# A graph network on one Trainium2 core: VectorE's sums moved ahead of the reads of PSUM

## The chip, the cores and the metric

The kernel runs on one core of a Trainium2 chip. The metric is the device time of a whole execution in microseconds (us), as a median of several runs. A profile is one execution taken by the hardware profiler; its times are counted from the first instruction, and its span (631.9 us) is a little shorter than the execution's time (633.71 us), which also covers what lies around the instructions.

The engines are named as in the profile: PE is TensorE (matmul; PEld is its weight load), DVE is VectorE, ACT is ScalarE, POOL is GpSimd, SP issues the transfers.

## The reference, cut to what matters

`x` has 16 batches of 1024 nodes with 64 features, `adj` is 1024 x 1024, all float32. Layer 0 is an attention whose softmax runs over the queries and whose scores are multiplied by `adj`; layer 1 adds up five terms with `adj` and its square.

```python
# layer 0
Q, K, V = x @ Wq.T + bq, x @ Wk.T + bk, x @ Wv.T
score = softmax(einsum('bnc,bmc->bnm', Q, K), axis=1)
x = layernorm(x + einsum('bnm,bmc->bnc', einsum('bnm,mc->bnc', score, adj), V))
# layer 1, with both supports equal to adj
x_stack = [x]
for support in (adj, adj):
    x1 = einsum('ij,bjk->bik', support, x)
    x2 = 2.0 * einsum('ij,bjk->bik', support, x1) - x
    x_stack += [x1, x2]
x = layernorm(x + einsum('bnf,fo->bno', concatenate(x_stack), weight) + bias)
```

The kernel folds the weights of layer 1 first, so that layer 1 is two products with `adj`, called hop 1 and hop 2 here. `Y` is multiplied by `adj` and added to `U` (hop 1); the sum is multiplied by `adj` again and added to a third term (hop 2); a layer norm and the output follow. One more such product, ahead of the attention, is not touched.

## The kernel before: the parts that matter

Each hop is a product of a 1024 x 1024 matrix (left, `adj`) and a 1024 x 1024 matrix (right, nodes by batches and features). It is done with seven products of quarters in place of eight (Strassen's scheme in Winograd's form): sums of quarters of the left matrix (`S`) and of the right one (`T`) are made by VectorE, the seven products by TensorE, and each product is added to one or two quarters of the result. Products 2, 3 and 4 are split once more in the same way, into seven *parts* each; VectorE makes their eight inner sums (`halves`). Products 1, 5, 6 and 7 are done in two *groups* (`g` = 0 and 1) of eight matmuls.

The sums wait in one list. `later` puts them there, `fill(n)` takes out the first n and issues them on VectorE, `need` issues until those named are out.

```python
    line = []
    def later(name, pieces):
        line.extend((name, piece) for piece in pieces)
    def fill(n):
        for _ in range(min(n, len(line))):
            line.pop(0)[1]()
    def need(*names):
        while any(name in names for name, _ in line):
            fill(1)
```

A group is multiplied into a PSUM tile of two banks; then VectorE reads the tile, adding it to the result (`take`). A part goes into one bank of two tiles (`two_tiles`). Parts 1, 6, 7 and 4 use the same bank and parts 6, 7 and 4 add to what is in it, so part 6 has to wait until part 1 has been read, and so on; part 2 uses the other tile's first bank, parts 5 and 3 its second.

```python
        def take(self, pt, block, n, pair, m):
            # ... cut: cells and views ...
            if cells <= self.seen:
                nc.vector.tensor_add(at(self.res), got, at(self.res))
            elif self.plus is None:
                nc.scalar.activation(at(self.res), got, AF.Copy)
            else:
                nc.vector.tensor_add(at(self.res), got, at(self.plus))
            self.seen |= cells

        def targets(self, name):              # which quarters of the result
            return {
                1: [(0, 0)], 2: [(0, 0)], 3: [(0, 1)], 4: [(1, 0)], 6: [(0, 1)],
                5: [(1, 1)] + [(0, 1)] * (3 in self.twice),
                7: [(1, 1)] + [(1, 0)] * (4 in self.twice),
            }[name]

        def step(self, name, g, fills=0, rows=(0, 1)):
            self.matmuls(name, g, rows)       # tiles[g] for 1, 6, 7, 4; tiles[2 + g] for 2, 3, 5
            self.read(name, g, rows)
            fill(fills)

        def part(self, name, q, two_tiles):
            a, b = self.sub[q]
            tile_, bank = {1: (0, 0), 6: (0, 0), 7: (0, 0), 4: (0, 0), 2: (1, 0)}.get(q, (1, 1))
            pt = two_tiles[tile_][:, ts(bank, H)]
            # ... cut: four matmuls of 128 x 256 into pt ...
            self.take(pt, i * HB + 2 * di, 2, c * NP // 2 + 2 * dc, 2)

    PARTS = (1, 2, 6, 5, 7, 3, 4)
```

Hop 1 begins while the attention's last normalisation and weights are done (`weigh`, `transposed`), with products 1 and 2; products 5, 3, 6 and 7 are in `turns`, which both hops use; product 4 comes last.

```python
    hop_1.read(1, 0)
    two = (h[2], h[3])
    hop_1.part(2, 1, two)
    fill(1)
    hop_1.part(2, 2, two)
    fill(1)
    transposed(p, h[1])
    # ... cut: parts 6 and 5 with fill(1), parts 7, 3, 4 without, and weigh between them ...
    need("S1")
    line[:0] = [("T1", f) for f in hop_1.right_sum(1)]
    hop_1.step(1, 1, 7)
    two = (h[1], h[3])
    SUB_DONE = {2: (0, 0), 7: (1, 1), 3: (0, 1), 4: (1, 0)}

    def turns(product, room, after_5, after_6):
        S = product.S
        need("S1", "T1")
        lefts, rights = product.halves(3, room[0])
        later("half", [f for both in zip(lefts, rights) for f in both])
        for g in range(2):
            product.step(5, g, 6)
        need("half")
        later("T2", product.right_sum(2))
        later("T3", product.right_sum(3))
        for q in PARTS:
            product.part(3, q, two)
            fill(1)
        need("S2", "T2")
        if after_5:
            later("S3", left_sum(S, 3))
        lefts, rights = product.halves(4, room[1])
        later("half", lefts)
        for g in range(2):
            product.step(6, g, 5)
            after_6(g)
        need("S3", "T3")
        later("T4", product.right_sum(4))
        later("half", rights)
        for g in range(2):
            product.step(7, g, 4 if after_5 else 5)
            if not after_5:
                leave(1, 1, g)
        need("half")
```

A *leave* is the end of the layer norm for rows and columns of the result that are complete: ScalarE squares them, VectorE reduces the squares, the inverse root is made by GpSimd (`inverse_root`) or by ScalarE and VectorE (`inverse_root_2`), GpSimd (the last one: VectorE) multiplies, SP sends. All behind the square is put at the front of the list of sums.

```python
    def leave(i, c, g, half=None):
        # ... cut: r, the rows ...
        nc.scalar.activation(sq, r, AF.Square)
        def rest():
            engine = nc.gpsimd
            if half is not None and i:
                rstd = inverse_root_2(rows, 2 * nb)
                if (g, half) == (1, 0):
                    engine = nc.vector
            else:
                rstd = inverse_root(row_sums(rows, 2 * nb), 2 * nb)
            # ... cut: the product with rstd on engine, and two transfers out ...
        line.insert(0, ("leave", rest))

    # hop 2
    for g in range(2):
        hop_2.step(1, g, 6)
    need("half")
    for q in PARTS:
        hop_2.part(2, q, two)
        fill(1)
        if q in SUB_DONE:
            leave(0, 0, *SUB_DONE[q])
    turns(hop_2, room[::-1], False, lambda g: leave(0, 1, g))
    for q in PARTS:
        hop_2.part(4, q, two)
        fill(1)
        if q in SUB_DONE:
            leave(1, 0, *SUB_DONE[q])
    need("leave")
```

Of the kernel before, what the change touches and what calls it, by code (L numbers as in the profile page):

```python
# [18 lines left out]
def gnn_kernel(  # L19
# [31 lines left out]
    def ps_tile(name):  # L51
        return ps.tile([P, 2 * H], FP, tag="ps", name=name)
# [182 lines left out]
# [11 lines that stand above are left out]
    class Product:  # L246
# [87 lines left out]

        def step(self, name, g, fills=0, rows=(0, 1)):
            self.matmuls(name, g, rows)
            self.read(name, g, rows)
            fill(fills)

        def halves(self, name, room):  # L340

# [20 lines left out]
            ]  # L362
            return lefts, rights

        def part(self, name, q, two_tiles):


            a, b = self.sub[q]
            tile_, bank = {1: (0, 0), 6: (0, 0), 7: (0, 0), 4: (0, 0), 2: (1, 0)}.get(q, (1, 1))
            pt = two_tiles[tile_][:, ts(bank, H)]  # L370
            start = q in (1, 2, 5)
            W = H // 2
            for i in range(2):
                for k in range(2):
                    nc.tensor.matmul(  # L375
                        pt[:, ts(i, W)], a[:, k, ts(i, P)], b[:, :, k],
                        start=(start and i == k == 0), stop=(k == 1), skip_group_check=True,
                    )
            (i, c), = self.targets(name)
            di, dc = {1: (0, 0), 2: (0, 0), 6: (0, 1), 3: (0, 1), 7: (1, 1), 5: (1, 1), 4: (1, 0)}[q]  # L380
            self.take(pt, i * HB + 2 * di, 2, c * NP // 2 + 2 * dc, 2)

    PARTS = (1, 2, 6, 5, 7, 3, 4)
# [9 lines left out]
    def scores(n):  # L393

        p, m = steps[n]
        sc = [ps_tile(f"sc{j}") for j in range(2)]
        for h in range(2):
            for j in range(2):
                s = slice(j * C, (j + 1) * C)
                nc.tensor.matmul(  # L400
                    sc[j][:, ts(h, H)], GY[s, p, ts(m, P)], xT[s, p, ts(h, H)],
                    start=True, stop=True,
                )
        NM[n] = small.tile([P, 2], FP, tag="nm", name="nm")
        E[n] = att.tile([P, 2, N], FP, tag="e", name="e", bufs=3)
        for j in range(2):
            nc.vector.tensor_scalar(  # L407
                E[n][:, j], sc[j], -1.0, None, op0=ALU.mult, op1=ALU.min,
                accum_out=NM[n][:, j : j + 1],
            )  # L410
        SM[n] = small.tile([P, 2], FP, tag="es", name="es")

    def exponentials(n, j):
        nc.scalar.activation(  # L414
            E[n][:, j], E[n][:, j], AF.Exp, bias=NM[n][:, j : j + 1], scale=-1.0,
            accum_out=SM[n][:, j : j + 1],
        )

    def scaled(n):

        p, m = steps[n]
        ri = small.tile([P, 2], FP, tag="ri", name="ri")
        nc.vector.reciprocal(ri, SM.pop(n))
        US[n] = small.tile([P, 2, C], FP, tag="us", name="us")
        nc.vector.tensor_tensor(  # L425
            US[n], U[:, m, ts(p, P)].rearrange("p (b c) -> p b c", b=2),
            ri[:, :, None].to_broadcast([P, 2, C]), ALU.mult,
        )

    def weighted(n):  # L430
        p, m = steps[n]
        if m == 0:
            ACC[p] = pacc.tile([P, N], FP, tag="acc", name="acc")
        es, us = E.pop(n), US.pop(n)
        for h in range(2):
            for j in range(2):
                nc.tensor.matmul(  # L437
                    ACC[p][j * C : (j + 1) * C, ts(h, H)], us[:, j], es[:, j, ts(h, H)],
                    start=(m == 0), stop=(m == K8 - 1),
                )  # L440
# [96 lines left out]
    for n, (p, m) in enumerate(steps):  # L537
        if p == NP - 1:
            if m == 0:
                later("half", [f for both in zip(*hop_1.halves(2, room[0])) for f in both])  # L540
            fill(1)
        if n + 2 <= last:
            scores(n + 2)
            exponentials(n + 2, 0)
        if p and m > 4:
            weigh(p - 1, m - 5)
        elif p > 1 and m == 0:
            weigh(p - 2, 3)
        if n + 1 <= last:
            scaled(n + 1)  # L550
        weighted(n)
        if m == K8 - 1:
            take(p)
        if n + 2 <= last:
            exponentials(n + 2, 1)
        if p:
            if m == 0:
                norm_1(p - 1)
            elif m == 1:
                norm_2(p - 1)  # L560
            elif m == 4:
                transposed(p - 1)
# [7 lines left out]
    h = [pacc.tile([P, N], FP, tag="acc", name="h0")] + [ps_tile(f"h{n}") for n in (1, 2, 3)]  # L570
# [7 lines left out]
    hop_1.read(1, 0)  # L578
    two = (h[2], h[3])
    hop_1.part(2, 1, two)  # L580
    fill(1)
    hop_1.part(2, 2, two)
    fill(1)
    transposed(p, h[1])
    hop_1.part(2, 6, two)
    fill(1)
    hop_1.part(2, 5, two)
    fill(1)
    weigh(p, 0, h[1])
    hop_1.part(2, 7, two)  # L590
    hop_1.part(2, 3, two)
# [7 lines left out]
# [11 lines that stand above are left out]
        for g in range(2):  # L610
            product.step(5, g, 6)
        need("half")
        later("T2", product.right_sum(2))
        later("T3", product.right_sum(3))
        for q in PARTS:
            product.part(3, q, two)
            fill(1)
        need("S2", "T2")
        if after_5:
            later("S3", left_sum(S, 3))  # L620
# [13 lines that stand above are left out]
# [5 lines left out]
    ])  # L639
    for q in PARTS:  # L640
        hop_1.part(4, q, two)
        fill(1)
    need("S1")

    def leave(i, c, g, half=None):

        first_block = i * HB + 2 * g
        nb, b0 = (B // 2, c * B // 2) if half is None else (B // 4, c * B // 2 + half * B // 4)
        r = R[:, first_block : first_block + 2, b0 * C : (b0 + nb) * C].rearrange(
            "p i (b c) -> p i b c", c=C  # L650
        )
        sq = att.tile([P, 2, nb, C], FP, tag="rT", name="sq2")
        nc.scalar.activation(sq, r, AF.Square)  # L653
        rows = sq.rearrange("p i b c -> p (i b) c")

        def rest():
            engine = nc.gpsimd
            if half is not None and i:
                rstd = inverse_root_2(rows, 2 * nb)
                if (g, half) == (1, 0):  # L660
                    engine = nc.vector
            else:
                rstd = inverse_root(row_sums(rows, 2 * nb), 2 * nb)
            engine.tensor_tensor(
                r, r, rstd.rearrange("p (i b) c -> p i b c", i=2), ALU.mult
            )
            for n in range(2):
                nc.sync.dma_start(out[ts(first_block + n, P), b0 : b0 + nb], r[:, n])

        line.insert(0, ("leave", rest))  # L670

    hop_2 = Product(S, by_pair(U), by_pair(R), hop_1.tiles, xT.rearrange("p q (k f) -> p q k f", k=K8), (2, 3, 4))
    later("T1", hop_2.right_sum(1))
    lefts, rights = hop_2.halves(2, room[0])
    later("half", [f for both in zip(lefts, rights) for f in both])
    for g in range(2):
        hop_2.step(1, g, 6)
    need("half")
    for q in PARTS:
        hop_2.part(2, q, two)  # L680
        fill(1)
        if q in SUB_DONE:
            leave(0, 0, *SUB_DONE[q])
    turns(hop_2, room[::-1], False, lambda g: leave(0, 1, g))
    for q in PARTS:
        hop_2.part(4, q, two)
        fill(1)
        if q in SUB_DONE:
            leave(1, 0, *SUB_DONE[q])
    need("leave")  # L690
# [40 lines left out]
```

## Time and profile before

| what | us |
|---|---|
| time, median of three runs | 633.69 (632.64 to 634.97) |
| span of the profiled execution | 631.9 |
| TensorE busy | 606.1 |
| VectorE busy | 391.5 |
| ScalarE busy | 226.2 |
| GpSimd busy | 84.2 |

A row of the profile has a line of the kernel, the engine, the operation, what it writes and reads, and the busy time; a bracket or a last column says how long the engine was idle just before and what ended that. In the rows that matter here, L322 is a matmul of a group, L375 of a part, L309 and L313 are reads of a product by VectorE, L276 sums of the right matrix, L224 of the left one, L356 to L361 the inner sums of a product that is split again. `h` is a PSUM tile of the products, `U`, `GY` are results, `S`, `T` and `xs` hold sums. A float32 matmul has two records in the trace, so the four matmuls of a part count as x8 and the eight of a group as x16. The clock row gives the clock that TensorE was granted, in tenths of full speed. Ends of matmuls are modelled by the profiler.

### The profile page before, as it was taken

The page shows a single profiled execution, that of the slowest core. Times are in us where ns is not written, and L with a number is a line of the kernel's source. Part 1 is how long each engine was busy: PE and PEld are TensorE (multiplying, and loading weights), DVE is VectorE, ACT ScalarE, POOL GpSimd, SP SyncE. Part 2 cuts the span into 40 slices and gives each one's busy share as a digit, 9 for nine tenths or more (in the row PEclk, how much of TensorE's full clock was granted, in tenths as well). Part 3 has the DMA queues.
Part 4 walks back from the last instruction along what each step waited for, and adds up shares of the span by engine and source line. Part 5 has one row for each costly group of instructions (what it writes and reads, how often), then busy time and mean ns, then how long its engine had stood idle before and what let it go on. Part 6 is the DMA issues. An engine that isn't in the chain of part 4 may idle for free.

```text
span 631.9 us, 6267 instructions
## 1 busy us (share of the span) xinstructions
PE 606.1 (96%) x2414; PEld 297.0 (47%) x2414; DVE 391.5 (62%) x706; ACT 226.2 (36%) x381; POOL 84.2 (13%) x47
## 2 busy tenths in 40 slices
PE   9999999999999999999999999999879989899974
PEld 7544444433344343443434344476355464646453
DVE  1695321267767777676776869653675575475584
ACT  4110100256666676676767666621000000100111
POOL 0000022400020303020030303000000000420373
PEclk9999999999999999999999999999989999899988
DMA  8600001000000000000000000000000000010023
GB/s 306 245 1 1 0 0 66 1 0 2 0 2 1 0 1 1 2 1 0 1 1 1 2 1 0 1 0 2 0 1 0 0 1 0 25 43 1 13 81 106
DMA packets 7917, 14.32 MB, mean 23 GB/s; under 512 B 2128, under 2 KB 4176, under 8 KB 7888
## 3 DMA queue, kind: packets, MB, share of 16 engines
q1 hardware_dynamic: 7568, 13.90, 6.1%
q8 instruction: 19, 0.31, 0.2%
q14 instruction: 10, 0.08, 0.0%
q10 hardware_dynamic: 320, 0.03, 0.0%
HBM read 9.73 MB, written 4.19 MB: 22 GB/s over the span
## 4 chain that ended last, share of the span: by engine, by line
PE 90%; DVE 7%; DMA 1%; issue 1%; ACT 1%; POOLq 0%; POOL 0%; ACTq 0%
PE h L322 32%; PE sc L400 20%; PE acc L437 19%; PE h L375 10%; PE pw L473 3%; PE po L452 2%; PE pt L109 2%; PE pg L131 2%; DVE U L309 1%; DVE GY L313 1%; DMA xs<-in_x_dram 1%; DVE xs L360 1%; DVE xs L361 1%; DVE xs L357 1%; PE h L473 1%
## 5 line engine op out<-in xcount | busy, mean ns | idle before, releaser
L407 DVE TENSOR_SCALAR_CACHE_REDUCE e<-sc 128x1024 f32<-128x1024 f32 x128 | 151.6, 1221 | 64.9 <-PE sc L400 64.9
L414 ACT ACTIVATE e<-e,nm 128x1024 f32<-128x1024 f32 x128 | 146.2, 1142 | 75.4 <-DVE e L407 75.2
L400 PE MATMUL sc<-xT,GY 64*128 64x512 f32 x512 | 128.5, 615 | 0.5 <-DVE e L407 0.5
L437 PE MATMUL acc<-e,us 128*64 128x512 f32 x512 | 124.0, 605 | 0.3 <-DVE us L425 0.3
L185 POOL TENSOR_TENSOR rstd<-var,expo 128x16 f32<-128x16 f32 (+1 forms) x15 | 40.0, 2664 | 433.6 <-DVE var L180 433.5
L322 PE MATMUL h<-T,S 128*128 128x512 f32 x192 | 83.6, 593 | 2.8 <-DVE T L276 2.0
L400 PEld LDWEIGHTS sc<-xT,GY 64*128 64x128 f32 x512 | 45.1, 186 | 73.3 <-issue 49.7
L309 DVE TENSOR_TENSOR U<-h,U 128x512 f32<-128x512 f32 (+1 forms) x39 | 36.1, 935 | 63.6 <-PE h L322 52.6
L653 ACT ACTIVATE sq<-GY 128x512 f32<-128x512 f32 (+1 forms) x12 | 9.2, 770 | 173.8 <-DVE GY L309 151.5
L437 PEld LDWEIGHTS acc<-e,us 128*64 128x64 f32 x512 | 31.1, 136 | 71.0 <-issue 61.3
L322 PEld LDWEIGHTS h<-T,S 128*128 128x128 f32 x192 | 36.4, 190 | 48.0 <-issue 46.3
L375 PE MATMUL h<-xs 128*128 128x256 f32 x144 | 39.1, 436 | 10.9 <-DVE GY L309 5.9
L322 PE MATMUL h<-S,aT 128*128 128x512 f32 x96 | 41.7, 593 | 0.0
L311 ACT ACTIVATE U<-h 128x1024 f32<-128x1024 f32 (+1 forms) x9 | 8.4, 928 | 91.4 <-PE h L322 91.4
L375 PEld LDWEIGHTS h<-xs 128*128 128x128 f32 x144 | 31.1, 220 | 18.4 <-DVE GY L309 7.1
L309 DVE TENSOR_TENSOR GY<-h,GY 128x512 f32<-128x512 f32 (+1 forms) x25 | 19.3, 772 | 24.8 <-PE h L322 13.1
L322 PEld LDWEIGHTS h<-S,aT 128*128 128x128 f32 x96 | 18.3, 190 | 22.9 <-issue 22.7
L526 POOL TENSOR_TENSOR xs<-xs,mu 128x1024 f32<-128x1024 f32 x8 | 15.0, 1903 | 102.6 <-DVE T L276 90.2
L322 PE MATMUL h<-xs,aT 128*128 128x512 f32 x64 | 27.6, 592 | 0.0
L473 PEld LDWEIGHTS pw<-raw,xT 64*128 64x128 f32 x224 | 19.2, 187 | 15.8 <-issue 5.8
L414 ACT ACTIVATION_READ_ACCUMULATOR e<-e,nm 128x1 f32 x128 | 24.0, 188 | 0.0
L473 PE MATMUL pw<-raw,xT 64*128 64x192 f32 x224 | 24.0, 332 | 0.0
(142 smaller groups left out, 578.0 us busy)
## 6 DMA issues: line engine op xcount, KB each, us to landing
aT<-in_adjT_dram SPq DMA_DIRECT2D x8, 512.0 KB, 11.2
xs<-in_x_dram SPq DMA_DIRECT2D x7, 512.0 KB, 6.6
out_dram<-GY SPq DMA_DIRECT2D x16, 128.0 KB, 2.0
out_dram<-GY SPq DMA_DIRECT2D x8, 256.0 KB, 2.2
aT<-in_adjT_dram SPq DMA_DIRECT2D x1, 1024.0 KB, 5.0
xs<-in_x_dram SPq DMA_DIRECT2D x2, 256.0 KB, 2.8
w1s<-in_w_dram SPq DMA_DIRECT2D x2, 80.0 KB, 9.9
wq<-in_wqT_dram ACTq DMA_DIRECT2D x2, 16.0 KB, 3.1
```

Source lines behind the costliest of these rows:

```text
L109: nc.tensor.transpose(pt[:, ts(k, P)], xs[:, p, k, :], ident)
L131: nc.tensor.matmul(pg[:, ts(h, H)], m_w, xT[:, p, ts(h, H)], start=True, stop=True)
L185: nc.gpsimd.tensor_tensor(rstd, var, expo[:, 0:g], ALU.pow)
L309: nc.vector.tensor_add(at(self.res), got, at(self.res))
L322: nc.tensor.matmul(pt[:, ts(i, H)], a[:, k, ts(2 * g + i, P)], b[:, :, k], start=(start and k == 0), stop=(k == HB - 1), skip_group_check= ...
L375: nc.tensor.matmul(pt[:, ts(i, W)], a[:, k, ts(i, P)], b[:, :, k], start=(start and i == k == 0), stop=(k == 1), skip_group_check=True,)
L400: nc.tensor.matmul(sc[j][:, ts(h, H)], GY[s, p, ts(m, P)], xT[s, p, ts(h, H)], start=True, stop=True,)
L407: nc.vector.tensor_scalar(E[n][:, j], sc[j], -1.0, None, op0=ALU.mult, op1=ALU.min, accum_out=NM[n][:, j : j + 1],)
L414: nc.scalar.activation(E[n][:, j], E[n][:, j], AF.Exp, bias=NM[n][:, j : j + 1], scale=-1.0, accum_out=SM[n][:, j : j + 1],)
L437: nc.tensor.matmul(ACC[p][j * C : (j + 1) * C, ts(h, H)], us[:, j], es[:, j, ts(h, H)], start=(m == 0), stop=(m == K8 - 1),)
L473: nc.tensor.matmul(pw[:, j, ts(k, 3 * C)], xT[s, p, ts(2 * c + k, P)], raw[s, 0:3].rearrange("p w c -> p (w c)"), start=True, stop=True,)
L526: nc.gpsimd.tensor_tensor(rows_of(p), rows_of(p), mu[:, p, :, None].to_broadcast([P, G, C]), ALU.subtract)
```

## The change

VectorE's queue is in the order of the program. Before, a sum was put into it behind the read of a group or part, so that it ran only after the matmuls of that group had ended, though VectorE had been idle during them. The change puts the sums ahead of the read, so that they run beside the matmuls. For hop 1's product 2 this gives each of the seven parts a sum, where four had one. In hop 2, product 1's second group goes between products 5 and 3, product 2's second and later parts get no single sums, and the first quarter's leaves are two of a whole group in place of four; two of the last four leaves take GpSimd's power in place of ScalarE's square root.

```diff
         def step(self, name, g, fills=0, rows=(0, 1)):
             self.matmuls(name, g, rows)
+            fill(fills)
             self.read(name, g, rows)
-            fill(fills)

-        def part(self, name, q, two_tiles):
+        def part(self, name, q, two_tiles, fills=1):
 ...
+            fill(fills)
             (i, c), = self.targets(name)
 ... the fill(1) behind every part is dropped; in the attention's last pair
 ... fill(1) moves from the head of a turn to just before weighted(n)

     def turns(product, room, after_5, after_6):
         for g in range(2):
             product.step(5, g, 6)
         need("half")
+        if not after_5:
+            product.step(1, 1, 1)
+            leave(0, 0, 1)
         later("T2", product.right_sum(2))

     def leave(i, c, g, half=None):
-            if half is not None and i:
+            if half is not None and i and g != half:
                 rstd = inverse_root_2(rows, 2 * nb)
-                if (g, half) == (1, 0):
+                if g:
                     engine = nc.vector

-    for g in range(2):
-        hop_2.step(1, g, 6)
+    hop_2.tiles = [h[0], h[2], h[3], h[1]]
+    hop_2.step(1, 0, 9)
+    hop_2.part(2, 1, two)
+    hop_2.part(2, 2, two)
     need("half")
-    for q in PARTS:
+    for q in PARTS[2:]:
         hop_2.part(2, q, two)
-        fill(1)
-        if q in SUB_DONE:
-            leave(0, 0, *SUB_DONE[q])
+    leave(0, 0, 0)
```

More of the change, by code (lines that the diff above doesn't have):

```diff
@@ L550, in gnn_kernel @@
             scaled(n + 1)
+        fill(1)
         weighted(n)
@@ L580, in gnn_kernel @@
     hop_1.part(2, 1, two)
-    fill(1)
     hop_1.part(2, 2, two)
-    fill(1)
     transposed(p, h[1])
     hop_1.part(2, 6, two)
-    fill(1)
     hop_1.part(2, 5, two)
-    fill(1)
     weigh(p, 0, h[1])
@@ L616, in turns @@
             product.part(3, q, two)
-            fill(1)
         need("S2", "T2")
@@ L641, in gnn_kernel @@
         hop_1.part(4, q, two)
-        fill(1)
     need("S1")
@@ L675, in gnn_kernel @@
     later("half", [f for both in zip(lefts, rights) for f in both])
-    for g in range(2):
-        hop_2.step(1, g, 6)
+    hop_2.tiles = [h[0], h[2], h[3], h[1]]
+    hop_2.step(1, 0, 9)
+    hop_2.part(2, 1, two)
+    hop_2.part(2, 2, two)
     need("half")
-    for q in PARTS:
+    for q in PARTS[2:]:
         hop_2.part(2, q, two)
-        fill(1)
-        if q in SUB_DONE:
-            leave(0, 0, *SUB_DONE[q])
+    leave(0, 0, 0)
     turns(hop_2, room[::-1], False, lambda g: leave(0, 1, g))
@@ L686, in gnn_kernel @@
         hop_2.part(4, q, two)
-        fill(1)
         if q in SUB_DONE:
```

## The prediction

> **What bounds the kernel now.** I read the page first: how busy each engine is, and where in the span TensorE (PE) is not.
>
> ```profile
> PE 606.1 (96%) x2414; PEld 297.0 (47%) x2414; DVE 391.5 (62%) x706; ACT 226.2 (36%) x381; POOL 84.2 (13%) x47
> ...
> PE   9999999999999999999999999999879989899974
> ...
> PEclk9999999999999999999999999999989999899988
> ```
>
> TensorE is busy 96% of the span, so nothing can be won but its gaps. They all lie in the last 190 us (slices 29 to 40), which are the two hops, and in three places the clock row dips too. The change touches just this stretch. Next, the waits of TensorE alone from 430 us to the end:
>
> ```profile
> PE h L375 <- DVE GY L309: 5.9, 3, 3.5
> PE h L375 <- DVE U L309: 5.7, 3, 2.8
> PE h L322 <- DVE T L276: 2.0, 1, 2.0
> PE h L322 <- DVE GY L309: 0.8, 1, 0.8
> PE h L375 <- DVE GY L313: 0.8, 1, 0.8
> ```
>
> Columns: total, times, longest. All nine waits, 15.1 us, are for VectorE: mostly for a read of a PSUM tile (L309, L313), once for a sum (L276). The timeline of TensorE says when; the bracket is the idle time ahead of the row:
>
> ```profile
> 445.40 13.97 PE L322 MATMUL h<-T,S 128*128 128x512 f32 x32 [2.01 <-DVE T L276]
> ...
> 461.82 2.00 PE L375 MATMUL h<-GY,S 128*128 128x256 f32 x8 [0.72 <-DVE U L309]
> 466.63 7.13 PE L375 MATMUL h<-xs 128*128 128x256 f32 x24 [2.81 <-DVE U L309]
> ...
> 510.26 5.45 PE L375 MATMUL h<-xs 128*128 128x256 f32 x24 [2.12 <-DVE U L309]
> ...
> 538.42 7.13 PE L375 MATMUL h<-xs 128*128 128x256 f32 x24 [2.07 <-DVE GY L309]
> ...
> 549.79 14.00 PE L322 MATMUL h<-T,S 128*128 128x512 f32 x32 [0.78 <-DVE GY L309]
> ...
> 566.29 2.00 PE L375 MATMUL h<-U,S 128*128 128x256 f32 x8 [0.77 <-DVE GY L313]
> 568.69 5.45 PE L375 MATMUL h<-xs 128*128 128x256 f32 x24 [0.41 <-DVE GY L309]
> ...
> 611.97 8.27 PE L375 MATMUL h<-xs 128*128 128x256 f32 x24 [3.45 <-DVE GY L309]
> ```
>
> A part shows as x8 and a group as x16. Three parts (x24) take 5.45 us behind the wait at 510.26, but 7.13 and 8.27 us behind three others. There the clock was at half:
>
> ```profile
> 466.00:467.00 1.00, 0.37 (x2) 1.00 0.00 0
> ...
> 468.00:469.00 1.00, 1.00 (x4) 0.50 0.00 0
> ```
>
> (The column before the last two is the granted clock.) What VectorE did ahead of 466.63, from its timeline:
>
> ```profile
> 459.41 2.35 DVE L309 TENSOR_TENSOR U<-h,U 128x1024 f32<-128x1024 f32 x2 [0.71 <-PE h L322]
> 461.68 0.68 DVE L360 TENSOR_TENSOR xs<-GY 128x512 f32<-128x512 f32 x1
> ...
> 465.89 0.68 DVE L309 TENSOR_TENSOR U<-h,U 128x512 f32<-128x512 f32 x1
> ```
>
> Seven sums, 461.68 to 465.89, stand between the read of product 5's second group and the read of part 1, and part 6 adds into part 1's bank, so it waits. It was idle 0.71 us just before, while TensorE ran: the sums are not too many, they are late.
>
> [...] The trace agrees on the half (0.50) and on its length (467.2 to 471.0, 539.4 to 542.7), but idle times of 2.07 and 2.81 us brought it, while 2.01 and 2.12 us did not[...]. [...] the trace has a sum (L357) of 1.53 us in place of 0.68 at 562.44, beside GpSimd's product of 562.28.
>
> **The units.** From consecutive starts in the timelines: a part 1.73 us (473.60, 475.32, 477.05), a group of eight matmuls 6.87 (477.05 to 490.78 for two); a VectorE sum or half-width read 0.60, a full read 1.14. A read starts 1.93 us after its part's start and 7.15 after its group's. A wait also costs some 0.16 us of drain (two parts at 504.52 show 3.62 against 3.46). So before, the nine waits cost 15.1 + 1.5 = 16.6 us, and the slow clock (6.97 - 5.19) twice, and 8.10 - 5.19: 6.5 us. In all TensorE loses 23.1 us there.
>
> **The change, part by part.** No matmul, read or sum is added or removed; only VectorE's order changes (one sum per read, ahead of it, a group's sums ahead of its read), product 1's second group moves, and the square roots and leaves of hop 2 are regrouped. I laid VectorE's new order against TensorE's with these units.
>
> Product 2, hop 1: the first S1 sum comes ahead of part 1's read, which ends at 424.18 and not 423.77; part 6 starts near 424.24, not 423.88. Loss 0.36. The parts now take three S2 sums as well.
>
> Product 5, hop 1: T1's four sums run from about 438 us, while product 1's second group is multiplied, and not after its read at 443.43. The 2.01 us wait goes; product 5 starts at 443.5.
>
> Product 3, hop 1: all eight sums are made before the last read of product 5. That read, two of 1.14 us, still holds part 2 back (it uses the same tile): the wait of 0.72 stays, 0.97 with drain. Part 1's read, one sum behind it, ends 0.5 us before part 6 can start. The wait of 2.81 and its slow window go.
>
> Product 4, hop 1: the four right sums come before product 7's second read. Behind it VectorE has 2.28 us of read, one sum (0.60) and part 1's read (0.68), against 3.46 us of parts 1 and 2: loss 0.46 in place of 2.12.
>
> Hop 2, products 1 and 2: nine pieces fit under the first group (from 513 or so, the read of product 4's last part, to 517.5: T1 2.4, five sums 3.0). Behind the read (1.14) come one sum and part 1's read: 2.4 us, under 3.46. The 2.07 wait and its slow window go.
>
> Product 1's second group now runs between products 5 and 3: 6.87 us in which product 5's second read (2.28) is done, so the 0.77 and 0.41 waits go, and the leaves that stood before product 5 (0.78) too. But its own read (1.23) is followed by a new thing: ScalarE's square (1.06), the reduction of it on VectorE (1.24 with the small scale) and only then part 1's read (0.68), as VectorE's queue is in order. 7.15 + 1.23 + 1.06 + 1.24 + 0.2 + 0.75 = 11.6 us from the group's start, against 6.87 + 3.46 = 10.3: new loss 1.2.
>
> Product 4, hop 2: before, two reads (2.27), a reduction, four sums and part 1's read gave the wait of 3.45. Now the sums come before the reads, but the square of the last leave (1.06) is waited for, with its reduction (1.3); the first reads begin 0.4 us late behind the sums. Loss 2.8 with drain, in place of 3.6.
>
> The end: the last part's read waits for a reduction, square root and reciprocal of the leave before it, some 1.2 us behind its matmuls; then 3.4 us of square, reduction, root and product, against 4.28 before (623.83 to 628.11), and the same 3.8 us to the end. From the last matmul that is 0.2 us longer.
>
> Losses after: 0.36 + 0.97 + 0.46 + 1.2 + 2.8 = 5.8. To this I add 0.5[...] and 1.4 for the clock at 2.8 us of idle[...]. With 0.2 for the end: 7.9 in place of 23.1, so 15.2; walking the starts forward instead gave 15.8. I take 15.5: 633.7 - 15.5 = 618.2 us.
>
> **Rivals.** First: the waits only move. A sum ahead of a read delays that read, and TensorE waits for reads; with every read so delayed 0.6 us, some 30 parts would cost 18 us and the kernel would be near 634. Against it: a part gives VectorE 1.73 us and it needs 1.2, and its timeline shows idle times of 0.44 ahead of the reads even now. Second: the leaves become the bound. A square and reduction between two reads costs 2.4 us at each of three places; the gain would shrink to 10 or so, 624 us. For it: GpSimd takes 3 us a power, and it and ScalarE sit inside the chain; against: only two places have a read behind them at once. Third: the slow clock stays at random places; two more slow windows make 621.7. Fourth: every wait including the last goes, with no slow window: 614.
>
> **Range and chances.** The first five places follow from order alone, and I trust them to 1 us together; the end is worth 2 us either way, a window 1.8. Eight times in ten between 615.4 and 622.0. Faster by over 2% means below 621.0; 2.8 us of error in one direction is needed to miss it: 0.84. Within 2%: 0.15. Slower: 0.01, as no added work is on the path.
>
> **What would show it.** In the changed trace TensorE's waits should be four or five, 5 to 6 us together, none over 1.5 before 590 us; no wait for T; product 5 of hop 1 at 443.5; the clock at half once at most, near 597 us; VectorE's sums of a group ended before its read. I am wrong if parts 6 or 2 wait at other places than those named, if the square of a leave holds VectorE over 1.5 us, or if the clock is at half twice.

## The result, and the profile after

The changed kernel takes 617.91 us (median of four, 616.33 to 619.28) against 634.33; the ratio is 0.973 (0.967 to 0.979). Run again beside the experiments it took 615.71 against 633.41, 0.972 (0.969 to 0.975). The span of its first profile is 617.1 us. First the page: busy TensorE, its slices and its clock.

```profile
PE 599.7 (97%) x2414; PEld 293.4 (48%) x2414; DVE 391.4 (63%) x702; ACT 225.4 (37%) x377; POOL 86.0 (14%) x45
...
PE   7999999999999999999999999999999999999994
...
PEclk8999999999999999999999999999999999999998
```

The gaps of slices 29 to 39 are gone, and the clock's dips with them (slice 40 is the end, where TensorE has nothing left to do). VectorE does what it did before (391.4 us against 391.5). A new gap stands in slice 1. The waits of TensorE for VectorE in the hops (total, times, longest; this view covers 405 us to the end) are 3.3 us in place of 15.1:

```profile
PE h L375 <- DVE GY L309: 2.2, 2, 1.1
PE h L375 <- DVE U L309: 1.1, 3, 0.7
```

Its timeline shows where each of them is, and where none is left:

```profile
446.94 13.90 PE L322 MATMUL h<-T,S 128*128 128x512 f32 x32
...
463.28 1.99 PE L375 MATMUL h<-GY,S 128*128 128x256 f32 x8 [0.72 <-DVE U L309]
465.11 5.34 PE L375 MATMUL h<-xs 128*128 128x256 f32 x24
...
505.02 5.45 PE L375 MATMUL h<-xs 128*128 128x256 f32 x24 [0.19 <-DVE U L309]
...
558.00 5.45 PE L375 MATMUL h<-xs 128*128 128x256 f32 x24 [1.07 <-DVE GY L309]
...
599.29 5.45 PE L375 MATMUL h<-xs 128*128 128x256 f32 x24 [1.14 <-DVE GY L309]
```

Product 5 (446.94) starts without a wait, part 6 of product 3 (465.11) too; three parts take 5.3 to 5.5 us everywhere, so the clock is never at half in the hops (1.00 granted from 405 to 607 us). VectorE's timeline at the place where seven sums stood behind the read of product 5:

```profile
458.15 0.69 DVE L361 TENSOR_TENSOR xs<-GY,xs 128x512 f32<-128x512 f32 x1
460.87 2.35 DVE L309 TENSOR_TENSOR U<-h,U 128x1024 f32<-128x1024 f32 x2 [2.04 <-PE h L322]
463.15 0.68 DVE L276 TENSOR_TENSOR T<-GY,T 128x512 f32<-128x512 f32 x1
463.75 0.68 DVE L309 TENSOR_TENSOR U<-h,U 128x512 f32<-128x512 f32 x1
```

The last inner sum starts at 458.15, so VectorE is idle for 2.04 us before the read; before, the read came first. VectorE ran in the order of the program: before, it was idle for 0.71 us ahead of the read at 459.41 with seven sums behind it, which in this profile ran ahead of the read. One sum stands between the read and part 1's read (463.75), where seven did.

By stretch: from the last normalisation of the attention (its sum on VectorE starts at 416.39 before, 419.69 after) to the end, 215.5 us became 197.4. So the hops gain 18.1 us, and everything ahead of them lost 3.3. That loss is at the input: TensorE's waits of the start in this profile have the line

```profile
PE pt L109 <- DMA xs<-in_x_dram: 3.1, 2, 2.2
```

against 0.2 us in all before. No line of the change touches the input; the first run below asks whether it is chance.

### The profile page after: what moved, and what is told of

It reads as the page before. It is cut to its first block, busy times and chain, and to the rows that moved or that the text cites. A ratio compares the mean times of both kernels' runs of the same rounds, so it can differ in the third digit from the quotient of the medians.

```text
span 617.1 us, 6253 instructions
## 1 busy us (share of the span) xinstructions
PE 599.7 (97%) x2414; PEld 293.4 (48%) x2414; DVE 391.4 (63%) x702; ACT 225.4 (37%) x377; POOL 86.0 (14%) x45
## 4 chain that ended last, share of the span: by engine, by line
PE 91%; DVE 5%; DMA 2%; ACT 1%; issue 1%; ACTq 0%; DVEq 0%
PE h L322 33%; PE sc L401 20%; PE acc L438 19%; PE h L375 8%; PE pw L474 3%; PE pt L109 2%; PE po L453 2%; PE pg L131 2%; DVE GY L309 1%; DMA xs<-in_x_dram 1%; DVE U L309 1%; ACT sq L651 1%; DMA wq<-in_wqT_dram 1%; PE h L474 1%; DVE var L179 1%
## 5 line engine op out<-in xcount | busy, mean ns | idle before, releaser
L185 POOL TENSOR_TENSOR rstd<-var,expo 128x16 f32<-128x16 f32 (+1 forms) x15 | 42.5, 2832 | 417.3 <-DVE var L180 417.3
L651 ACT ACTIVATE sq<-GY 128x1024 f32<-128x1024 f32 (+1 forms) x10 | 8.9, 887 | 159.3 <-DVE GY L309 159.3
L375 PE MATMUL h<-xs 128*128 128x256 f32 x144 | 32.7, 383 | 2.6 <-DVE GY L309 2.2
L375 PEld LDWEIGHTS h<-xs 128*128 128x128 f32 x144 | 27.0, 190 | 7.7 <-DVE GY L309 3.0
L474 PEld LDWEIGHTS pw<-raw,xT 64*128 64x128 f32 x224 | 19.2, 187 | 15.8 <-issue 5.8
```

Source lines behind the costliest of these rows:

```text
L185: nc.gpsimd.tensor_tensor(rstd, var, expo[:, 0:g], ALU.pow)
L375: nc.tensor.matmul(pt[:, ts(i, W)], a[:, k, ts(i, P)], b[:, :, k], start=(start and i == k == 0), stop=(k == 1), skip_group_check=True,)
L474: nc.tensor.matmul(pw[:, j, ts(k, 3 * C)], xT[s, p, ts(2 * c + k, P)], raw[s, 0:3].rearrange("p w c -> p (w c)"), start=True, stop=True,)
```

## The experiments

Nine runs, each timed in three or five rounds beside the kernel before on the same chip. Where nothing else is said, a diff is against the changed kernel.

**The changed kernel again.** No edit.

> The changed kernel once more, on the chip of the next three, to compare them with it. Its first profile had TensorE start late (3.3 us, a wait for the input at 8.8 us), in a stage that the change doesn't touch. Theory: that is chance, and this profile begins the hops near 410.8 us as the kernel before does, with 614 us of span and 616.5 of time. Rival: the change does it, and TensorE waits some 2 us at the start again, 618 to 619 us.

615.71 us (615.60 to 616.50), span 613.6. The line of the input is now

```profile
PE pt L109 <- DMA xs<-in_x_dram: 0.3, 1, 0.3
```

and the sum on VectorE that ends the attention starts at 416.24. The late start was chance, and the sum that the change moves in the attention's last turns brings nothing either (416.39 before); the waits in the hops are the same five. (In the profiles of this study the wait for the input lies between 0.2 and 3.1 us.)

**Sums ahead of the reads, nothing else of the change.**

```diff
-        if not after_5:
-            product.step(1, 1, 1)
-            leave(0, 0, 1)
 ...
-    hop_2.tiles = [h[0], h[2], h[3], h[1]]
-    hop_2.step(1, 0, 9)
-    hop_2.part(2, 1, two)
-    hop_2.part(2, 2, two)
+    for g in range(2):
+        hop_2.step(1, g, 6)
     need("half")
-    for q in PARTS[2:]:
+    for q in PARTS:
         hop_2.part(2, q, two)
-    leave(0, 0, 0)
+        if q in SUB_DONE:
+            leave(0, 0, *SUB_DONE[q])
```

The choice of root in `leave` is put back too.

> Sums ahead of the reads everywhere, but hop 2's order, its leaves and its square roots as before. Theory A (the place of the sums is the whole gain; moving product 1's second group only exchanges its waits of 0.8 and 0.4 for one of 1.1): within 1 us of the changed kernel, 616 to 618.5. Theory B (the move carries part of the gain): 2 to 4 us slower than the changed kernel, 620 to 622, with waits back ahead of hop 2's products 5 and 3.

618.58 us, 0.977 (0.973 to 0.980): 2.9 slower than the changed kernel beside it. That is the difference, and these are the waits, of theory B; its 620 to 622 us is missed, since the changed kernel itself came out at 615.7. The run puts back three things at once, the move, its leaves and the roots. By the two profiles 2.1 us of the difference are waits (2.44 and 0.72 in place of 1.07) and 0.5 the end (11.3 us from the last part's start against 10.8), where the roots differ too; what the roots are worth by themselves was not measured. The timelines show what the move with its leaves buys, first TensorE's, then VectorE's:

```profile
539.45 14.00 PE L322 MATMUL h<-T,S 128*128 128x512 f32 x32 [2.44 <-DVE GY L309]
```

```profile
537.29 0.69 DVE L179 TENSOR_REDUCE var<-sq 128x8 f32<-128x512 f32 x1 [0.76 <-ACT sq L648]
538.01 0.79 DVE L180 TENSOR_SCALAR var<-var 128x8 f32<-128x8 f32 x1
538.72 0.68 DVE L309 TENSOR_TENSOR GY<-h,GY 128x512 f32<-128x512 f32 x1
```

Four leaves are worked in among the parts of product 2, each ahead of a part's read: VectorE waits 0.76 us for ScalarE's square, and the read of the last part, ready long before, ends too late for product 5.

**The move alone, sums behind the reads.** Against the kernel before:

```diff
         need("half")
+        if not after_5:
+            product.step(1, 1, 1)
+            leave(0, 0, 1)
 ...
-    for g in range(2):
-        hop_2.step(1, g, 6)
+    hop_2.tiles = [h[0], h[2], h[3], h[1]]
+    hop_2.step(1, 0, 9)
+    # ... parts 1 and 2, need("half"), the other parts, each with fill(1) behind it; leave(0, 0, 0)
```

> The kernel before with only product 1's second group moved between products 5 and 3 of hop 2 (and the leaves that belong to it), sums still behind the reads. Theory A: no gain, since nine sums now stand between the first group's read and part 1's: 1.1 + 5.4 + 0.7 - 3.5 = a wait of 3.8 us in place of 2.1, and with the slow clock 634 to 637. Theory B (the move brings its own gain): 629 to 631.

633.33 us against 633.41, 1.000 (0.998 to 1.002), just under theory A's range: nine sums behind the first group's read do make part 6 wait for 3.88 us (it was 2.07), and the waits of 0.8, 0.8 and 0.4 are gone, which pays for it. The move with its leaves is worth nothing by itself, and with the roots 2.9 us once the sums stand ahead (1.6 us where the parts' sums are behind, from the runs of 611.64 and 613.22 below, which ran on two chips).

**Which sums? Groups' ahead, parts' behind.** The changed kernel with

```diff
-            fill(fills)
             (i, c), = self.targets(name)
 ...
             self.take(pt, i * HB + 2 * di, 2, c * NP // 2 + 2 * dc, 2)
+            fill(fills)
```

> The changed kernel, but a part's sum behind its read again; a group's sums stay ahead. Theory A2 (the gain is that of the groups' sums; ahead of a part's read a sum or a leave only delays TensorE): the waits of 1.1 us at product 3 and product 4 of hop 2 and the two of 0.2 go, 2.5 us and some drain, 613.5 to 615.5, so 2.5 to 3 us faster than the changed kernel. Theory B2 (the parts' sums must be ahead too, or the next sums come late): waits of 0.6 at parts, 2 us slower than the changed kernel or more.

611.64 us (611.25 to 612.33), 0.966 (0.963 to 0.968): 4.1 us better than the changed kernel, and better than either theory had it. TensorE waits for VectorE in the hops once, at part 2 of hop 1's product 3:

```profile
PE h L375 <- DVE U L309: 0.7, 1, 0.7
```

VectorE's timeline at hop 2's product 3 shows why the wait of 1.07 is gone:

```profile
550.95 0.69 DVE L309 TENSOR_TENSOR GY<-h,GY 128x512 f32<-128x512 f32 x1 [0.50 <-PE h L375]
551.63 1.22 DVE L179 TENSOR_REDUCE var<-sq 128x16 f32<-128x1024 f32 x1
```

Part 1's read goes first, and the leave's reduction, whose square ScalarE has finished by then, comes behind it. Theory A2 is right on the cause and low on the size, which it had at 2.5 to 3 us: the four waits with their drain are 3.2 us, the end is 0.5 shorter, and a delay of 0.3 beside GpSimd's product, told further down, is gone.

**The same split with hop 2 and leaves as before.** The run with sums ahead only, once with just the parts' sums ahead (`step` reads and then fills), once with just the groups' (`part` reads and then fills).

> As the run with sums ahead only (hop 2 and leaves as before), but only a part's sum is ahead of its read, a group's sums are behind it as in the kernel before. Theory A2 (the groups' sums are the gain, a part's sum ahead of its read costs): no gain, 634 to 638. Theory B2 (each place gives its share): 625 to 630.

> As the run with sums ahead only (hop 2 and leaves as before), but only a group's sums are ahead of its read, a part's sum is behind it. Theory A2: 3 to 4 us faster than the run with both, 614.5 to 616, as the leaves' squares no longer hold back a part's read. Theory B2: as that run or slower, 618.5 to 622.

639.67 us, 1.009 (1.006 to 1.012), and 613.22, 0.968 (0.965 to 0.971), both against 634.02. The groups' sums bring all of it, 20.8 us. The parts' sums ahead cost 5.6 on the kernel before, and 5.4 on top of the groups' sums (618.58 against 613.22, on two chips; 6.0 if each is counted from the kernel before beside it). In the first case TensorE's waits in the hops are 19.9 us against 15.1, the longest 6.3 (3.5 before), ahead of part 6 in product 4 of hop 2. A read with something in front of it is a read that TensorE may have to wait for. A leave comes out of the same list as the sums, and in this last comparison it is most of the cost: of 3.2 us of added waits, 2.8 stand at the two places where a leave is in front of the read (ahead of product 5 and in product 4 of hop 2), and 0.2 at each of two places where it is a sum alone.

**The clock.** The kernel before with idle matmuls (of zeros, into a bank that is written over later) where TensorE waited and then ran at half clock.

```diff
+    def busy(q, n):
+        if q == 2:
+            for _ in range(n):
+                nc.tensor.matmul(two[1][:, H : H + P], still, still, start=True, stop=True, skip_group_check=True)
 ...
             product.part(3, q, two)
+            if after_5:
+                busy(q, 11)
```

and so with 8 and 14 in hop 2's products 2 and 4.

> The kernel before with 11, 8 and 14 idle matmuls of 128 x 128 put where TensorE waited 2.8, 2.1 and 3.5 us and then ran at half clock (between parts 2 and 6 of hop 1's product 3, hop 2's products 2 and 4); the waits themselves stay. Theory C (the slow clock [...] costs 1.8 us a window, three windows in the profile before): no slow clock at those three places, 3.5 to 6.5 us off, 627 to 630. Rival (the slow clock costs nothing of its own, since VectorE sets the pace there): 632 to 635.

645.69 us, 1.019 (1.016 to 1.022): both theories missed, since the experiment was badly built. TensorE's timeline:

```profile
469.14 4.14 PE L389 MATMUL h<-still 128*128 128x128 f32 x22 [4.02 <-DVE U L309]
```

The idle matmuls waited themselves, for the read of part 2, whose tile (though not its bank) they write. Their time came on top: 3.9, 2.6 and 5.6 us to the next row, 12.1, for 11.7 measured. The two agree in part by chance, since the waits also grew by 4.8 us while the parts behind them, the clock being full for more of them, took 5.2 us less. The time says nothing of the clock's cost. Only in the last place is there a tile that is free at that time (again against the kernel before):

```diff
         hop_2.part(4, q, two)
+        if q == 2:
+            for _ in range(14):
+                nc.tensor.matmul(h[0][:, 0:P], still, still, start=True, stop=True)
```

> The kernel before with 14 idle matmuls only at the last place (hop 2's product 4, between parts 2 and 6), now into a tile that has been read long before, so that they don't wait themselves: 14 x 0.21 = 3.0 us of them in a wait of 3.5. Theory C ([...] the slow clock, which costs its own 1.8 to 2.9 us behind that wait): parts 6, 5 and 7 take 5.4 us and not 7 to 8, and the time is 1.8 to 3 us less, 631 to 632.5. Rival (the slow clock there costs nothing of its own): 633.5 to 634.5.

632.18 us against 632.67, 0.999 (0.997 to 1.000): no difference that is clear of zero. TensorE's timeline shows that the clock was kept, and what came instead:

```profile
609.89 1.99 PE L375 MATMUL h<-xs 128*128 128x256 f32 x8 [0.33 <-DVE GY L309]
612.72 3.72 PE L375 MATMUL h<-xs 128*128 128x256 f32 x16 [0.84 <-DVE GY L309]
```

Two parts take 3.7 us, so full speed, but a new wait of 0.84 stands ahead of part 5: VectorE's small scaling (L180) took 1.08 us (610.99) in place of 0.17 there, and it does so in the profile of the kernel before too (1.08 us at 613.08), hidden behind the slow matmuls. From part 6 to part 4 the profile before has 9.83 us (611.97 to 621.80), this one 8.11: 1.7 us less, as theory C has it. Over 22 runs against 27 the medians differ by only 0.5 us (632.18 lies in theory C's range because the kernel before was faster beside it, too), and the interval reaches from 1.8 us faster to 0.2 slower. So the times decide for neither theory.

The profiles say more, for the other two places as well, where no free tile was there. The clock is not slow at the same places in every execution, and where it stayed full behind the same wait, the stretch is shorter by 1.7 us: from part 6 of hop 1's product 3 to product 6, 10.42 us in the profile before (466.63 to 477.05) and 8.74 in the run with the move alone (466.59 to 475.33); from part 6 of hop 2's product 2 to product 5, 11.37 (538.42 to 549.79) and 9.69 in this run (538.03 to 547.72). So at each of these three places the slow clock costs 1.7 us of its own, at the last one with the new wait taken off. Whole executions agree in direction: of the 27 runs of the kernel before, the fastest (630.1 us) had a mean granted clock of 0.995 and the slowest (636.5 us) of 0.984.

**The last wait.** The variant with parts' sums behind, and part 2 in the second bank of part 1's tile.

```diff
-            tile_, bank = {1: (0, 0), 6: (0, 0), 7: (0, 0), 4: (0, 0), 2: (1, 0)}.get(q, (1, 1))
+            tile_, bank = {1: (0, 0), 6: (0, 0), 7: (0, 0), 4: (0, 0), 2: (0, 1)}.get(q, (1, 1))
```

> The variant with groups' sums ahead and parts' sums behind, with part 2 in the second bank of part 1's tile, so that it doesn't wait for the last read of product 5 in hop 1. Theory: the last wait on VectorE (0.72 us with 0.16 of drain) goes, 610.8 in place of 611.6, and TensorE waits for VectorE nowhere in the hops. Rival (the wait passes on to part 6, whose bank's read now comes behind the two reads of product 5): no change, 611.6.

625.93 us, 0.988 (0.986 to 0.991): 14 us worse than without it. Neither theory foresaw it. Part 2 now waits for part 1's read at all six split products (0.8 to 2.4 us), and part 6 for part 2's at five of them (0.8 each). Part 2 at the first:

```profile
424.72 1.99 PE L375 MATMUL h<-GY,aT 128*128 128x256 f32 x8 [2.38 <-DVE U L309]
```

Waits in this program go by tile, not by bank, as these 0.8 to 2.4 us show: a second tile, and not a second bank, is what lets part 2 start before part 1 has been read.

## Why the prediction was right, by its steps

618.2 us were predicted and 617.91 measured, but two errors helped. The hops' gain is 18.1 us by the profile, where 15.2 to 15.8 were worked out; and of the first four runs at least the profiled one (619.28 us) started late. With the second set of runs the gain is 17.7 us, 2.2 more than the 15.5 forecast. That the number came out within 0.3 us is luck; the mechanism, place by place, mostly is not:

- *What bounds the kernel; the sums are late, not too many*: right. With the same work on VectorE the waits went, and the groups' sums ahead do it alone (0.968).
- *Product 2, loss 0.36*: part 6 starts 0.35 us later, counted from the attention's last sum (7.84 against 7.49 us).
- *Product 5 starts at 443.5*: 443.48 in the second profile, 446.94 - 3.3 in the first.
- *Product 3, the wait of 0.72 stays, that of 2.81 goes*: so it is. *Product 4, loss 0.46*: 0.20 of idle time with 0.16 of drain.
- *Hop 2, products 1 and 2*: no wait. *New loss of 1.2 behind product 1's second group*: 1.07 with 0.16 of drain, by the chain that was given (square, reduction, part 1's read).
- *Hop 2's product 4, loss 2.8*: wrong by 1.5; 1.14 with drain is 1.3. The term that failed is the square's wait. I let it begin after both reads of product 7's second group, but the leave needs only the first. VectorE's rows, then ScalarE's:

```profile
594.74 1.22 DVE L309 TENSOR_TENSOR GY<-h,GY 128x1024 f32<-128x1024 f32 x1 [0.43 <-PE h L322]
595.88 1.21 DVE L313 TENSOR_TENSOR GY<-h,xT 128x1024 f32<-128x1024 f32 x1
597.21 1.22 DVE L179 TENSOR_REDUCE var<-sq 128x16 f32<-128x1024 f32 x1
```

```profile
596.05 1.06 ACT L651 ACTIVATE sq<-GY 128x1024 f32<-128x1024 f32 x1 [5.80 <-DVE GY L309]
```

  The square (596.05) runs beside the second read, and the reduction follows that read at once. The sums, which I had 0.4 us too late, were out before 594.3 for the same reason.
- *1.4 for the clock*, the author's estimate with stretches at half clock that cost 1.8 and 2.9 us in the profile before (6.97 - 5.19 and 8.10 - 5.19): not spent; with no wait over 1.14 us the clock stays full in the hops (1.00). (Of the slow clock's length the prediction read 3.8 and 3.3 us; the half clock of the profile before lasts 3.4 us both times, 467.5 to 470.9 and 539.2 to 542.6.)
- *0.5 for VectorE's sums beside GpSimd's products*, the author's estimate, with one sum of 1.53 us in place of 0.68 in the profile before: some 0.3. One sum takes 2.22 us in place of 0.68, beside GpSimd's product of 560.41 (1.90 us); why it is longer was not shown. It stands ahead of the read of part 5, in whose bank part 3 is to be written:

```profile
560.64 2.22 DVE L276 TENSOR_TENSOR T<-U,T 128x512 f32<-128x512 f32 x1
562.78 0.68 DVE L309 TENSOR_TENSOR GY<-h,GY 128x512 f32<-128x512 f32 x1
```

  Part 3 starts at 563.51, 5.51 us behind part 6, where the same step takes 5.28 at 599.29, and the next part loses another 0.1. The delay is too short to show as a wait. With the part's sum behind its read, a sum of 1.83 us (556.74) delays nothing.
- *The end 0.2 longer*: 0.7 (10.8 us from the last part's start, 10.1 before).
- The losses after are then 0.35 + 0.88 + 0.36 + 1.23 + 1.3 + 0.3 + 0.7 = 5.1 us where I had 7.9, and 23.1 - 5.1 = 18.0 agrees with the 18.1 of the profiles. The waits were forecast as 5 to 6 us together and are 3.3. The 6.5 us of clock in the 23.1 are those of the one execution that was profiled; how many slow stretches an execution has differs, as the profiles above show.
- *Rival one, reads delayed by the sums*: true of the parts, and 4.1 us of the changed kernel's time. Most of them lie in the losses that I worked out (0.36, 0.46, 1.2 and 2.8); I didn't ask what the other order would give. *Rival two, the leaves become the bound*: two of the waits that were left come from them, 2.2 us and not ten. *Rival three, the slow clock stays at random places*: not in the hops, in either profile. *Rival four, every wait goes*: not by this change; the variant with the parts' sums behind comes near, with one wait left and 611.64 us.

## What to carry to other kernels

On an engine that works in the order of the program, as VectorE did here (idle for 0.71 us with seven sums behind a read), and that both reads the accumulators and prepares operands, put preparation ahead of the read of a long block, whose matmuls hide it, and behind the read of a short block, for which the next matmul is waiting. Anything that waits for a third engine (here a square) goes behind the nearest read that TensorE needs. Ask of every place which is ready first: the item in front, or the read. (Shown here for blocks of 6.9 and 1.7 us with sums of 0.6; how long a block must be was not measured.)

## What was not expected of the hardware

In the prediction's profile the length of a wait alone does not decide whether the slow clock follows: it followed 2.07 and 2.81 us, and not 2.01 and 2.12. Other executions agree. The same wait of 2.8 us ahead of part 6 in hop 1 was followed by three parts in 7.13 us in the profile before and in 5.45 in the run with the move alone, whose 2.13 us at hop 1's product 4 were followed by the half clock instead:

```profile
466.59 5.45 PE L375 MATMUL h<-xs 128*128 128x256 f32 x24 [2.82 <-DVE U L309]
...
508.54 7.13 PE L375 MATMUL h<-xs 128*128 128x256 f32 x24 [2.13 <-DVE U L309]
```

In the hops of all profiles together TensorE had 26 waits of 2 us and more. The half clock followed all six of 3.45 to 6.29 us, and seven of the 20 between 2.01 and 2.87 us (2.07 in the profile before, not in the run of 632.18 us; 2.12 the other way round). It followed none of the shorter waits. What decides between 2.01 and 2.87 us was not shown. In the profile before the half clock begins at 467.5, 539.2 and 610.9 us and lasts 3.4, 3.4 and 6.8 us. The changed kernel's longest wait in the hops, 1.14 us, is below every wait that the half clock followed.
